# A triangle-multiplication layer and a gated row layer in one kernel: transfers of the opening reordered, stage-border copies and stores moved, one load split

## The chip, the cores and the metric

The kernel runs on one core of one Trainium2 chip. The metric is the device time of one execution in microseconds (us), and the median over several runs is compared. Profiles show one execution. TensorE (PE, with its weight loads PEld), VectorE (DVE), ScalarE (ACT) and GpSimd (POOL) compute; SyncE (SP) only issues transfers, and ScalarE and GpSimd can issue some too.

## The reference

The input x has 384 x 384 positions of 128 channels in float32. Two layers follow one another.

```python
def layernorm(x, g, b): ...                       # over the channels
z = layernorm(x, norm_g, norm_b)
left  = (z @ Wl + bl) * sigmoid(z @ Wlg + blg)
right = (z @ Wr + br) * sigmoid(z @ Wrg + brg)
core = einsum('bikh,bjkh->bijh', left, right)     # 128 products of 384 x 384 x 384
x1 = x + sigmoid(x @ Wg + bg) * (layernorm(core, onorm_g, onorm_b) @ Wout + bout)

l = x1 @ W_left + b_left + x1 @ W_eq + b_eq
rsum = sum over j of (x1 @ W_right + b_right)
u = l * rsum * sigmoid(x1 @ W_gate + b_gate)
y = layernorm(u @ W_out + b_out + x1, ln_scale, ln_bias)
```

## The kernel before, in words

The work runs in three stages, each bound to the order in which the program is written: every instruction goes through `seq`, so each engine executes its instructions in program order. Semaphores are set by the tile framework; a transfer waits for what it reads and for the buffer it overwrites.

**Stage 1 (0 to about 1140 us)** reads x in chunks of 8 rows i by 128 columns k (`load_chunk`, six buffers), computes mean and variance per position on VectorE (`stats`, lines 220 to 230), the power -1/2 on GpSimd (`powers`), the shifted rows z on GpSimd (`shift`), transposes them on TensorE and copies them with ScalarE (`front`, lines 258 to 264), and multiplies them with the joined weights `wz` (`back`, line 298). Four rows of a chunk are one step. The opening before the loop loads two chunks on SP; on ScalarE's queue it loads four weight matrices into `stage`, the norm's gain g and bias b as columns, the four bias vectors broadcast over the partitions, and four more chunks. `fold` (lines 152 to 156) and `weights` (line 162) fold gain and biases into `wz`: wz = g*W + bias/C + a mean of (b-g)*W, computed by one matmul p1.

**Stage 2 (about 1140 to 1885 us)** runs over the 128 values of h: it loads left and right of one h, forms the 384 x 384 product in PSUM (`pc`, line 449), copies it to `ct` with ScalarE, keeps sums over h for the second norm (`csum`, `csq`), and stores `ct` to the scratch tensor `core_d` in device memory, laid out [i, h, j]. The last h is treated by itself (lines 467 to 480): its first block of 128 rows is finished first, so that variance, square root, reciprocal and a Newton step (`variance`, `root`, `inverse`, `newton`) for rows 0 to 127 can run at once; the result is `roots[0][1]`, called r.

**Stage 3 (about 1885 us to the end)** runs over rows i in steps t, several rows in flight. Per row: the gate product (`front`, line 564), `scale_core` (cs = core times r: for rows 0 to 3 on VectorE, line 598, with r spread over the partitions by a matmul; later on GpSimd from `rt`, line 600), `layer0` (lines 609 to 612), `gated_left` (626 to 631), `layer1` (638, 639), statistics, normalization and store. Loads come in groups of four rows: `load_x`, `add_x` (a transfer issued by GpSimd that adds onto what `load_x` brought), and `load_core` (line 532 for `ct`, line 536 for `rt`). `store_rstd(0)` (line 557) writes r to device memory, from where `rt` reads it back. `pieces` are the variance and roots of row blocks 1 and 2, done a bit at a time between the rows: three variance operations or the like on ScalarE and GpSimd, or a reciprocal on VectorE.

The PSUM pools of stage 3 are `ps` (four banks) and `ps2` (four banks), opened in this order over the banks that stage 2 frees.

Of the kernel before, what the change touches and what calls it, by code (L numbers as in the profile page):

```python
# [8 lines left out]
F32 = mybir.dt.float32  # L9
# [10 lines left out]
def triangle_then_gated_row_kernel(ctx: ExitStack, tc: tile.TileContext, a: dict, out: bass.AP):  # L20
# [36 lines left out]
    def seq(ins):  # L57

        return tc.keep_in_program_order(ins)
# [7 lines left out]
    def column(name, queue=nc.sync):  # L67
        t = const([P, 1], "col_" + name)
        load(t, a[name].rearrange("(p o) -> p o", o=1), queue)
        return t  # L70
# [10 lines left out]
    with ExitStack() as ctx2:  # L81
# [15 lines left out]
        with tc.tile_pool(name="p1x", bufs=6, side="right") as xp, \  # L97
# [9 lines left out]
            loaded, normed = {}, {}  # L107
            lr, full = {}, []

            def load_chunk(n, queue=nc.sync):  # L110
                if n < len(chunks):
                    kb, ig, c = chunks[n]
                    i0 = ig * G + c * XR
                    xt = xp.tile([P, XR, C], F32, tag="xt", name="xt")
                    seq(queue.dma_start(
                        out=xt, in_=x[i0:i0 + XR, kb * P:(kb + 1) * P, :].rearrange("i k c -> k i c")
                    ))
                    loaded[n] = xt

            for n in range(2):  # L120
                load_chunk(n)

            stage = lrp.tile([P, H, G, 2], F32, tag="lr", name="stage").rearrange("p h i s -> p (h i s)")
            wst, bst = stage[:, 0:4 * H], stage[:, 4 * H:8 * H]
            m1, d = stage[:, 8 * H:9 * H], stage[:, 9 * H:9 * H + 1]
            sides = ("l", "r", "lg", "rg")
            for n, w in enumerate(sides):
                load(wst[:, n * H:(n + 1) * H], a["L0_conv_W" + w], nc.scalar)  # L130
            g0, b0 = column("L0_conv_norm_g", nc.scalar), column("L0_conv_norm_b", nc.scalar)
            for n, b in enumerate(sides):
                load(bst[:, n * H:(n + 1) * H], a["L0_conv_b" + b].partition_broadcast(P), nc.scalar)
            for n in range(2, 6):
                load_chunk(n, nc.scalar)
            ident = const([P, P], "ident")
            make_identity(nc, ident)
            avg = const([P, P], "avg")
            seq(nc.vector.memset(avg, 1.0 / P))
            mhalf = const([P, 16], "mhalf")  # L140
            seq(nc.vector.memset(mhalf, -0.5))

            warm = const([P, 1], "warm")
            seq(nc.scalar.activation(warm, mhalf[:, 0:1], AF.Sigmoid))
            wz = const([P, 4 * H], "wz")
            p1 = pps.tile([P, 2, 4 * H], F32, tag="pr", name="p1")[:, 0]

            def fold():

                seq(nc.vector.tensor_sub(d, b0, g0))
                seq(nc.vector.tensor_scalar(m1, avg, d, None, ALU.mult))
                seq(nc.tensor.matmul(p1, lhsT=m1, rhs=wst, start=True, stop=True))
                seq(nc.vector.tensor_scalar(bst, bst, 1.0 / C, None, ALU.mult))
                seq(nc.vector.scalar_tensor_tensor(wst, wst, g0, bst, ALU.mult, ALU.add))

            def weights():

                for g in range(2):  # L160
                    gs = slice(g * 2 * H, (g + 1) * 2 * H)
                    seq(nc.vector.tensor_add(
                        wz[:, gs].rearrange("p (h s) -> p s h", s=2),
                        wst[:, gs].rearrange("p (s h) -> p s h", s=2),
                        p1[:, gs].rearrange("p (s h) -> p s h", s=2),
                    ))

            wc = const([P, C], "wc")
# [154 lines left out]
            for k in range(AHEAD):  # L323
                for half in range(2):
                    stats(*steps[k], half)
                if k < AHEAD - 1:
                    powers(*steps[k])
                if k == 0:
                    fold()
                    zs[0] = shift(*steps[0])  # L330
                    front(*steps[0], zs.pop(0))
                if k == 1:
                    weights()
                    zs[1] = shift(*steps[1])
            for k, (n, q) in enumerate(steps):
                if k + 2 < len(steps):
                    zs[k + 2] = shift(*steps[k + 2])
                if k + AHEAD - 1 < len(steps):
                    powers(*steps[k + AHEAD - 1])
                for half in range(2):  # L340
                    back(n, q, half)
                    if half == 0 and k + 1 < len(steps):
                        front(*steps[k + 1], zs.pop(k + 1))
                    if k + AHEAD < len(steps):
                        stats(*steps[k + AHEAD], half)
                if q == NQ - 1:
                    del loaded[n], normed[n]
                    load_chunk(n + 6)
                    if chunks[n][2] == G // XR - 1:
                        store_nd(*chunks[n][:2])  # L350
                store_zt(n, q)
                store_slice()
                if k == 4:
                    for t, src in later:
                        load(t, src)
                if k == 20:
                    m2 = late_weights()
                if k == 21:
                    late_products(m2)
                if k == len(steps) - 2 * G // 4 + 16:  # L360
                    assert not full
                    for h in range(2):
                        load_h(h)
# [43 lines left out]
        with tc.tile_pool(name="p2r", bufs=2, side="right", reuse_waits="tile") as rrp, \  # L407
# [28 lines left out]
            for h in range(H):  # L436
# [20 lines left out]
                if h < H - 1:  # L457
                    seq(nc.scalar.copy(ct, pc[:, :, :N]))  # L458
                    seq(nc.scalar.activation(sq, ct, AF.Square))
                    seq(nc.vector.tensor_add(csum, csum, ct))  # L460
                    seq(nc.vector.tensor_add(csq, csq, sq))
                    load_h(h + 3)

                    queue = nc.sync if h < H - 3 else nc.scalar
                    seq(queue.dma_start(out=to, in_=ct))
                else:
                    seq(nc.scalar.copy(ct[:, 0], banks[0]))
                    seq(nc.scalar.activation(sq[:, 0], ct[:, 0], AF.Square))
                    seq(nc.scalar.dma_start(out=to[:, 0], in_=ct[:, 0]))
                    seq(nc.vector.tensor_add(csum[:, 0], csum[:, 0], ct[:, 0]))  # L470
                    seq(nc.vector.tensor_add(csq[:, 0], csq[:, 0], sq[:, 0]))
                    variance(0, slice(0, N))
                    root(0)
                    inverse(0, slice(0, N))
                    newton(0, slice(0, N))
                    seq(nc.scalar.copy(ct[:, 1:], pc[:, 1:, :N]))
                    seq(nc.scalar.dma_start(out=to[:, 1:], in_=ct[:, 1:]))
                    seq(nc.gpsimd.tensor_tensor(sq[:, 1:], ct[:, 1:], ct[:, 1:], ALU.mult))
                    seq(nc.gpsimd.tensor_tensor(csum[:, 1:], csum[:, 1:], ct[:, 1:], ALU.add))
                    seq(nc.gpsimd.tensor_tensor(csq[:, 1:], csq[:, 1:], sq[:, 1:], ALU.add))  # L480
# [5 lines left out]
    with ExitStack() as ctx3:  # L486
# [3 lines left out]
        xp, fp, inp, op = pool("p3x", 6), pool("p3f", A + 4), pool("p3in", 3), pool("p3out", 3)  # L490
        wp, sp = pool("p3w", 4), pool("p3s", 4)
        lp = pool("p3l", 11)
        ps, ps2 = pool("p3ps", 4, space=PSUM), pool("p3ps2", 4, space=PSUM)

        def bank(name):
            return ps.tile([P, 512], F32, tag="bank", name=name)
# [32 lines left out]
        def load_core(i0):  # L529
            if i0 < N:  # L530
                ct = inp.tile([P, RG, N], F32, tag="ct", name="ct")
                seq(nc.sync.dma_start(out=ct, in_=core_d[i0:i0 + RG].rearrange("i h j -> h i j")))
                rt = None
                if i0 > 0:
                    rt = inp.tile([P, RG, N], F32, tag="rt", name="rt")
                    seq(nc.sync.dma_start(
                        out=rt.rearrange("p i j -> p (i j)"),
                        in_=rstd_d[i0:i0 + RG].rearrange("i j -> (i j)").partition_broadcast(P),
                    ))
                cin[i0] = ct, rt  # L540
# [160 lines left out]
                ))  # L701
            stores.clear()

        for i0 in range(0, 4 * RG, RG):
            load_x(i0)
        load_core(0)
        store_rstd(0)
        load_core(RG)

        pieces = [(variance, b, s) for b in range(1, NB) for s in cols]  # L710
# [3 lines left out]
        for t in range(N + 3):  # L714
# [6 lines left out]
            if t >= 2 and fetched <= f + 16:  # L721
                load_x(fetched)
                fetched += RG
            if t >= 7 and added <= f + 8:
                add_x(added)
                added += RG
            if t < N:
                scale_core(t)
            if t >= 16 and t % 5 == 0 and pieces:
                step, b, s = pieces.pop(0)  # L730
                step(b, s)
                if step is root:
                    step, b, s = pieces.pop(0)
                    step(b, s)
                if step is newton and s == cols[-1]:
                    store_rstd(b)
# [70 lines left out]
```

## Time and profile before

| | us |
|---|---|
| median of three runs | 3308.44 (3307.75 to 3309.41) |
| the profiled execution | 3307.08 |
| its span (first to last instruction) | 3305.3 |
| granted TensorE clock | 0.997 of full speed |

The span is 1.8 us shorter than the execution's own time. The costliest groups of the page show how the time is spent:

```profile
L298 PE MATMUL pr<-wz,zt 128*128 128x512 f32 x2304 | 1040.3, 593 | 6.2 <-DVE st L228 6.2
L449 PE MATMUL pc<-rr,lrh 128*128 128x384 f32 x2304 | 745.0, 487 | 2.7 <-POOL rr L428 2.7
L600 POOL TENSOR_TENSOR cs<-ct,rt 128x384 f32<-128x384 f32 x380 | 403.7, 1064 | 10.4 <-DMA rt<-rstd_d 9.6
```

Such a line gives the source line, engine and operation, result and operands, shape and count; after the first bar the busy time in us and the mean of one in ns; after the second the idle time of the engine just before these instructions and what ended most of it. The chain of work that ended last is TensorE's almost throughout: line 449 alone is 22% of the span, and lines 638, 609, 627, 564 and 626 have about 7% each.

### The profile page before, as it was taken

The page shows a single profiled execution, that of the slowest core. Times are in us where ns is not written, and L with a number is a line of the kernel's source. Part 1 is how long each engine was busy: PE and PEld are TensorE (multiplying, and loading weights), DVE is VectorE, ACT ScalarE, POOL GpSimd, SP SyncE. Part 2 cuts the span into 40 slices and gives each one's busy share as a digit, 9 for nine tenths or more (in the row PEclk, how much of TensorE's full clock was granted, in tenths as well). Part 3 has the DMA queues.
Part 4 walks back from the last instruction along what each step waited for, and adds up shares of the span by engine and source line. Part 5 has one row for each costly group of instructions (what it writes and reads, how often), then busy time and mean ns, then how long its engine had stood idle before and what let it go on. Part 6 is the DMA issues. An engine that isn't in the chain of part 4 may idle for free.

```text
span 3305.3 us, 48361 instructions
## 1 busy us (share of the span) xinstructions
PE 3267.0 (99%) x12486; PEld 1992.0 (60%) x12486; DVE 2495.4 (75%) x8041; ACT 1940.4 (59%) x4055; POOL 2247.9 (68%) x3295
## 2 busy tenths in 40 slices
PE   8999999999999999999999999999999999999998
PEld 4544444444444466666666666666777777777776
DVE  6777777777777655555555688888888888888888
ACT  4555555555555433343334467777777777777776
POOL 5555555555555455555555579889888888888887
PEclk9999999999999999999999999999999999999999
DMA  5999999999999499999999999999999999999983
GB/s 151 267 281 268 266 279 272 264 282 271 263 279 275 130 283 283 283 281 283 284 283 282 287 296 267 264 273 276 269 280 270 275 271 276 273 272 277 271 258 113
DMA packets 922818, 873.96 MB, mean 264 GB/s; under 512 B 25008, under 2 KB 837680, under 8 KB 922544
## 3 DMA queue, kind: packets, MB, share of 16 engines
q1 hardware_dynamic: 902480, 794.13, 78.3%
q0 software_dynamic: 13248, 72.36, 11.1%
q10 hardware_dynamic: 6816, 4.39, 0.5%
q8 instruction: 102, 1.67, 0.2%
q14 instruction: 172, 1.41, 0.1%
HBM read 508.89 MB, written 361.89 MB: 263 GB/s over the span
## 4 chain that ended last, share of the span: by engine, by line
PE 62%; POOL 1%; ACT 1%; DVE 1%; issue 0%; POOLq 0%; DVEq 0%; ACTq 0%
PE pc L449 22%; PE py L638 7%; PE pr L609 7%; PE pl L627 7%; PE pg L564 7%; PE pg L626 7%; PE py L639 4%; POOL rs L658 0%; ACT py L673 0%; POOL yt L690 0%; PE pxt L575 0%; PE pq L586 0%; POOL cs L600 0%; DVE st L653 0%; ACT gT L566 0%
## 5 line engine op out<-in xcount | busy, mean ns | idle before, releaser
L298 PE MATMUL pr<-wz,zt 128*128 128x512 f32 x2304 | 1040.3, 593 | 6.2 <-DVE st L228 6.2
L305 ACT ACTIVATE sg<-pr,rs 128x256 f32<-128x256 f32 x1152 | 482.7, 470 | 499.2 <-PE pr L298 365.6
L449 PE MATMUL pc<-rr,lrh 128*128 128x384 f32 x2304 | 745.0, 487 | 2.7 <-POOL rr L428 2.7
L307 DVE SCALAR_TENSOR_TENSOR lr<-pr,rs,sg 128x256 f32<-128x256 f32 x1152 | 505.0, 480 | 267.2 <-ACT sg L305 218.8
L298 PEld LDWEIGHTS pr<-wz,zt 128*128 128x128 f32 x2304 | 414.4, 190 | 417.1 <-issue 346.0
L449 PEld LDWEIGHTS pc<-rr,lrh 128*128 128x128 f32 x2304 | 452.7, 197 | 295.0 <-POOL rr L428 3.3
L673 ACT ACTIVATE py<-py,nm,rs 128x128 f32<-128x128 f32 x1149 | 492.8, 429 | 191.6 <-POOL rs L662 126.9
L638 PEld LDWEIGHTS py<-wo,u 128*128 128x128 f32 x2304 | 377.1, 191 | 100.6 <-DVE yt L684 0.6
L460 DVE TENSOR_TENSOR csum<-csum,ct 128x1152 f32<-128x1152 f32 x127 | 175.6, 1383 | 346.6 <-ACT ct L458 346.6
L600 POOL TENSOR_TENSOR cs<-ct,rt 128x384 f32<-128x384 f32 x380 | 403.7, 1064 | 10.4 <-DMA rt<-rstd_d 9.6
L428 POOL COPY rr<-lrh 128x768 f32<-128x768 f32 x128 | 183.1, 1430 | 329.4 <-DMA lrh<-lr_d 309.2
L458 ACT COPY ct<-pc 128x1152 f32<-128x1152 f32 x127 | 142.1, 1119 | 449.4 <-PE pc L449 449.4
L638 PE MATMUL py<-wo,u 128*128 128x128 f32 x2304 | 402.7, 275 | 0.3 <-ACT wo L620 0.3
L690 POOL TENSOR_TENSOR yt<-yt,lnb 128x384 f32<-128x384 f32 x380 | 400.6, 1056 | 2.1 <-DVE yt L684 2.0
L653 DVE BATCH_NORM_STATS2 st<-py 128x6 f32<-128x128 f32 x1152 | 266.3, 287 | 84.6 <-PE py L639 82.9
L243 POOL TENSOR_SCALAR sd<-mv 128x8 f32<-128x8 f32 (+1 forms) x145 | 28.6, 197 | 436.7 <-DVE mv L230 436.6
L253 POOL TENSOR_TENSOR z<-xt,nd 128x512 f32<-128x512 f32 x288 | 299.8, 1041 | 35.9 <-POOL z L253 30.6
L609 PE MATMUL pr<-cs,wc 128*128 128x384 f32 x768 | 315.1, 492 | 0.1
L627 PE MATMUL pl<-x1T,mat_L_conv_W_left 128*128 128x384 f32 x768 | 311.4, 487 | 3.5 <-ACT gT L566 3.4
L639 PE MATMUL py<-ident,x1T 128*128 128x128 f32 x1152 | 314.0, 273 | 0.0
L626 PE MATMUL pg<-x1T,mat_L_conv_W_gate 128*128 128x384 f32 x768 | 310.8, 486 | 1.2 <-ACT g L629 1.0
L564 PE MATMUL pg<-xt,mat_L_conv_Wg 128*128 128x384 f32 x736 | 298.4, 487 | 0.0
(119 smaller groups left out, 4892.6 us busy)
## 6 DMA issues: line engine op xcount, KB each, us to landing
lr_d<-lr SPq DMA_DIRECT2D x128, 1024.0 KB, 7.1
lrh<-lr_d SPq DMA_DIRECT2D x128, 768.0 KB, 7.8
xt_d<-zt SPq DMA_DIRECT2D x288, 256.0 KB, 5.5
ct<-core_d SPq DMA_DIRECT2D x96, 768.0 KB, 4.8
rt<-rstd_d SPq DMA_DIRECT2D x95, 768.0 KB, 8.4
out_dram<-yt SPq DMA_DIRECT2D x94, 768.0 KB, 7.2
core_d<-ct SPq DMA_DIRECT2D x125, 576.0 KB, 8.9
xt<-in_x_dram SPq DMA_DIRECT2D x140, 512.0 KB, 7.0
```

The source lines that it names most:

```text
L298: seq(nc.tensor.matmul(pr[:, r, :], lhsT=zts[n, q][:, 2 * half + r, :], rhs=wz, start=True, stop=True))
L305: seq(nc.scalar.activation(sg[r], pr[:, r, 2 * H:], AF.Sigmoid, scale=rs[r]))
L307: seq(nc.vector.scalar_tensor_tensor(t[:, :, c * XR + r0 + r, :], pr[:, r, :2 * H].rearrange("k (h s) -> k h s", s=2), rs[r], sg[r].rearra ...
L449: seq(nc.tensor.matmul(banks[ib], lhsT=t[:, kb, ib * P:(ib + 1) * P, 0], rhs=rr[:, kb], start=(kb == 0), stop=(kb == NB - 1),))
L564: seq(nc.tensor.matmul(pg[:, :N], lhsT=wg0, rhs=r["xT"], start=True, stop=True))
L600: seq(nc.gpsimd.tensor_tensor(cs, ct[:, i % RG], rt[:, i % RG], ALU.mult))
L609: seq(nc.tensor.matmul(pr[:, :N], lhsT=wc, rhs=r["cs"], start=True, stop=True))
L626: seq(nc.tensor.matmul(pg2[:, :N], lhsT=wgate, rhs=r["x1T"], start=True, stop=True))
L627: seq(nc.tensor.matmul(pl[:, :N], lhsT=wleft, rhs=r["x1T"], start=True, stop=True))
L638: seq(nc.tensor.matmul(py[:, s], lhsT=r["u"][:, s], rhs=r["wo"], start=True, stop=False))
L639: seq(nc.tensor.matmul(py[:, s], lhsT=r["x1T"][:, s], rhs=ident, start=False, stop=True, is_transpose=True))
L673: seq(nc.scalar.activation(py[:, s], py[:, s], AF.Identity, bias=bias, scale=scale))
```

## The change

The edits fall into three places.

*Opening.* `load_chunk` can load a part of a chunk; SP loads the first four rows of chunk 0, then g and b as two rows of 128 numbers, the other four rows, and chunks 1 to 3. Chunks 4 and 5 are loaded after the first step of the loop. ScalarE's queue keeps the four weights only; the four bias vectors are loaded as one row each by GpSimd. `fold` stands between the two halves of the first statistics and brings g and b into columns by a small matmul with the identity; the bias goes into p1 by a second matmul with one row, and `weights` multiplies by g while adding p1. `busy` issues matmuls whose result nobody reads.

*Border between stages 2 and 3.* The first block's store of the last h is split into rows 0 to 3 and 4 to 127; ScalarE's copy of blocks 1 and 2 stands ahead of `variance` and `root`; r is stored by GpSimd's queue at this place instead of by SP in stage 3. The two PSUM pools of stage 3 change places. The core of rows 0 to 3 is loaded in two transfers, h 0 to 126 and h 127, and stands ahead of the fourth load of x.

*Row loop.* After t = 12 `add_x` is issued only where t mod 4 is 1, and pieces run where t mod 4 is 3, not where t is a multiple of 5.

```diff
-            def load_chunk(n, queue=nc.sync):
+            def load_chunk(n, part=slice(0, XR)):
...
-            for n in range(2):
-                load_chunk(n)
+            load_chunk(0, slice(0, 4))
...
+            for n, v in enumerate(("g", "b")):
+                load(gb[n:n + 1], a["L0_conv_norm_" + v].rearrange("(o h) -> o h", o=1))
             for n, w in enumerate(sides):
                 load(wst[:, n * H:(n + 1) * H], a["L0_conv_W" + w], nc.scalar)
-            g0, b0 = column("L0_conv_norm_g", nc.scalar), column("L0_conv_norm_b", nc.scalar)
-            for n, b in enumerate(sides):
-                load(bst[:, n * H:(n + 1) * H], a["L0_conv_b" + b].partition_broadcast(P), nc.scalar)
-            for n in range(2, 6):
-                load_chunk(n, nc.scalar)
+            load_chunk(0, slice(4, XR))
+            for n in range(1, 4):
+                load_chunk(n)
...
+            for n, b in enumerate(sides):
+                load(brow[:, n * H:(n + 1) * H], a["L0_conv_b" + b].rearrange("(o h) -> o h", o=1), nc.gpsimd)
...
+            def busy(n):
+
+                for _ in range(n):
+                    seq(nc.tensor.matmul(
+                        pb, lhsT=avg, rhs=avg.unsqueeze(1).to_broadcast([P, 4, P]), start=True, stop=True
+                    ))
...
-                seq(nc.vector.tensor_sub(d, b0, g0))
+                busy(2)
+                seq(nc.tensor.matmul(pgb, lhsT=gb, rhs=ident[0:2, 0:2], start=True, stop=True))
+                seq(nc.vector.tensor_copy(g0, pgb[:, 0:1]))
+                seq(nc.vector.tensor_sub(d, pgb[:, 1:2], g0))
                 seq(nc.vector.tensor_scalar(m1, avg, d, None, ALU.mult))
-                seq(nc.tensor.matmul(p1, lhsT=m1, rhs=wst, start=True, stop=True))
-                seq(nc.vector.tensor_scalar(bst, bst, 1.0 / C, None, ALU.mult))
-                seq(nc.vector.scalar_tensor_tensor(wst, wst, g0, bst, ALU.mult, ALU.add))
+                busy(1)
+                seq(nc.tensor.matmul(p1, lhsT=m1, rhs=wst, start=True, stop=False))
+                seq(nc.tensor.matmul(p1, lhsT=avg[0:1, :], rhs=brow, start=False, stop=True))
+                busy(1)
...
+                if k == 0:
+                    for i in range(4, 6):
+                        load_chunk(i)
...
-                    seq(nc.scalar.dma_start(out=to[:, 0], in_=ct[:, 0]))
+                    seq(nc.scalar.dma_start(out=to[:RG, 0], in_=ct[:RG, 0]))
+                    seq(nc.scalar.dma_start(out=to[RG:, 0], in_=ct[RG:, 0]))
...
+                    seq(nc.scalar.copy(ct[:, 1:], pc[:, 1:, :N]))
                     variance(0, slice(0, N))
                     root(0)
                     inverse(0, slice(0, N))
                     newton(0, slice(0, N))
-                    seq(nc.scalar.copy(ct[:, 1:], pc[:, 1:, :N]))
                     seq(nc.scalar.dma_start(out=to[:, 1:], in_=ct[:, 1:]))
+
+
+                    seq(nc.gpsimd.dma_start(out=rstd_d[0:P, :], in_=roots[0][1]))
...
-        ps, ps2 = pool("p3ps", 4, space=PSUM), pool("p3ps2", 4, space=PSUM)
+        ps2, ps = pool("p3ps2", 4, space=PSUM), pool("p3ps", 4, space=PSUM)
...
-                seq(nc.sync.dma_start(out=ct, in_=core_d[i0:i0 + RG].rearrange("i h j -> h i j")))
+
+                for hs in (slice(0, H),) if i0 > 0 else (slice(0, H - 1), slice(H - 1, H)):
+                    seq(nc.sync.dma_start(out=ct[hs], in_=core_d[i0:i0 + RG, hs].rearrange("i h j -> h i j")))
...
-        for i0 in range(0, 4 * RG, RG):
+        for i0 in range(0, 3 * RG, RG):
             load_x(i0)
         load_core(0)
-        store_rstd(0)
+        load_x(3 * RG)
         load_core(RG)
...
-            if t >= 7 and added <= f + 8:
+            if t >= 7 and (t % 4 == 1 or t < 12) and added <= f + 8:
...
-            if t >= 16 and t % 5 == 0 and pieces:
+            if t >= 16 and t % 4 == 3 and pieces:
```

More of the change, by code (lines that the diff above doesn't have):

```diff
@@ L113, in load_chunk @@
                     i0 = ig * G + c * XR
[L114 to L118, printed above, removed]
-            for n in range(2):
-                load_chunk(n)
+                    if part.start == 0:
+                        loaded[n] = xp.tile([P, XR, C], F32, tag="xt", name="xt")
+                    src = x[i0:i0 + XR, kb * P:(kb + 1) * P, :].rearrange("i k c -> k i c")
+                    seq(nc.sync.dma_start(out=loaded[n][:, part], in_=src[:, part]))
+            load_chunk(0, slice(0, 4))
             stage = lrp.tile([P, H, G, 2], F32, tag="lr", name="stage").rearrange("p h i s -> p (h i s)")
-            wst, bst = stage[:, 0:4 * H], stage[:, 4 * H:8 * H]
-            m1, d = stage[:, 8 * H:9 * H], stage[:, 9 * H:9 * H + 1]
+            wst, brow, gb = stage[:, 0:4 * H], stage[0:1, 4 * H:8 * H], stage[0:2, 8 * H:9 * H]
+            m1, d = stage[:, 9 * H:10 * H], stage[:, 10 * H:10 * H + 1]
             sides = ("l", "r", "lg", "rg")
+            for n, v in enumerate(("g", "b")):
+                load(gb[n:n + 1], a["L0_conv_norm_" + v].rearrange("(o h) -> o h", o=1))
             for n, w in enumerate(sides):
                 load(wst[:, n * H:(n + 1) * H], a["L0_conv_W" + w], nc.scalar)
-            g0, b0 = column("L0_conv_norm_g", nc.scalar), column("L0_conv_norm_b", nc.scalar)
-            for n, b in enumerate(sides):
-                load(bst[:, n * H:(n + 1) * H], a["L0_conv_b" + b].partition_broadcast(P), nc.scalar)
-            for n in range(2, 6):
-                load_chunk(n, nc.scalar)
-            ident = const([P, P], "ident")
-            make_identity(nc, ident)
+            load_chunk(0, slice(4, XR))
+            for n in range(1, 4):
+                load_chunk(n)
             avg = const([P, P], "avg")
@@ L141, in triangle_then_gated_row_kernel @@
             seq(nc.vector.memset(mhalf, -0.5))
+            ident = const([P, P], "ident")
+            make_identity(nc, ident)
+            for n, b in enumerate(sides):
+                load(brow[:, n * H:(n + 1) * H], a["L0_conv_b" + b].rearrange("(o h) -> o h", o=1), nc.gpsimd)
             warm = const([P, 1], "warm")
@@ L146, in triangle_then_gated_row_kernel @@
             p1 = pps.tile([P, 2, 4 * H], F32, tag="pr", name="p1")[:, 0]
+            pb = pps.tile([P, 2, 4 * H], F32, tag="pr", name="pb")[:, 0]
+            pgb = tps.tile([P, 4, P], F32, tag="pt", name="pgb")[:, 0, 0:2]
+            g0 = const([P, 1], "g0")
+            def busy(n):
[3 more added lines that the diff above has]
+                    ))
             def fold():
-                seq(nc.vector.tensor_sub(d, b0, g0))
+                busy(2)
+                seq(nc.tensor.matmul(pgb, lhsT=gb, rhs=ident[0:2, 0:2], start=True, stop=True))
+                seq(nc.vector.tensor_copy(g0, pgb[:, 0:1]))
+                seq(nc.vector.tensor_sub(d, pgb[:, 1:2], g0))
                 seq(nc.vector.tensor_scalar(m1, avg, d, None, ALU.mult))
-                seq(nc.tensor.matmul(p1, lhsT=m1, rhs=wst, start=True, stop=True))
-                seq(nc.vector.tensor_scalar(bst, bst, 1.0 / C, None, ALU.mult))
-                seq(nc.vector.scalar_tensor_tensor(wst, wst, g0, bst, ALU.mult, ALU.add))
+                busy(1)
+                seq(nc.tensor.matmul(p1, lhsT=m1, rhs=wst, start=True, stop=False))
+                seq(nc.tensor.matmul(p1, lhsT=avg[0:1, :], rhs=brow, start=False, stop=True))
+                busy(1)
             def weights():
@@ L161, in weights @@
                     gs = slice(g * 2 * H, (g + 1) * 2 * H)
-                    seq(nc.vector.tensor_add(
+                    seq(nc.vector.scalar_tensor_tensor(
                         wz[:, gs].rearrange("p (h s) -> p s h", s=2),
-                        wst[:, gs].rearrange("p (s h) -> p s h", s=2),
-                        p1[:, gs].rearrange("p (s h) -> p s h", s=2),
+                        wst[:, gs].rearrange("p (s h) -> p s h", s=2), g0,
+                        p1[:, gs].rearrange("p (s h) -> p s h", s=2), ALU.mult, ALU.add,
                     ))
@@ L325, in triangle_then_gated_row_kernel @@
                     stats(*steps[k], half)
+                    if k == 0 and half == 0:
+                        fold()
                 if k < AHEAD - 1:
@@ L328, in triangle_then_gated_row_kernel @@
                 if k == 0:
-                    fold()
                     zs[0] = shift(*steps[0])
+                    weights()
                     front(*steps[0], zs.pop(0))
                 if k == 1:
-                    weights()
                     zs[1] = shift(*steps[1])
```

## The prediction

> **What bounds the kernel now.** I read the page's busy table first, then the busy time by stage, TensorE's waits, and the order of time around the two places where TensorE stands idle.
>
> ```profile
> PE 3267.0 (99%) x12486; PEld 1992.0 (60%) x12486; DVE 2495.4 (75%) x8041; ACT 1940.4 (59%) x4055; POOL 2247.9 (68%) x3295
> ...
> 0.00:25.00 25.00, 9.96 (x22) 4.70 (x23) 11.56 (x64) 4.11 (x8) 10.48 (x23) 1.00 0.72 189
> ...
> 1880.00:1890.00 10.00, 7.60 (x29) 5.09 (x28) 7.89 (x9) 6.71 (x11) 2.06 (x2) 0.91 0.99 296
> ...
> 2020.00:2100.00 80.00, 77.38 (x367) 53.69 (x366) 66.67 (x239) 60.44 (x139) 68.72 (x95) 1.00 0.90 261
> 2100.00:2200.00 100.00, 98.48 (x470) 69.07 (x469) 87.43 (x305) 71.94 (x167) 89.46 (x127) 1.00 0.94 271
> ```
>
> The stage rows give the stretch, then busy us of PE, PEld, DVE, ACT, POOL. TensorE is idle 38 us of 3305.3. Of these 15.0 lie before 25 us, 2.4 at 1880 to 1890, 4.1 between 2020 and 2200, and about 14 after 3280, which nothing here touches. So the edits can win some 20 us at most, and only where TensorE waits; a new wait on its path costs its full length.
>
> ```profile
> 14.43 0.43 DVE L155 TENSOR_SCALAR stage<-stage 128x512 f32<-128x512 f32 x1 [5.63 <-DMA stage<-in_L_conv_brg_dram]
> 15.95 1.28 ACT L144 ACT_TABLE_LOAD   x1 [15.95 <-DMA xt<-in_x_dram]
> 17.35 0.57 ACT L264 COPY zt<-pt 128x512 f32<-128x512 f32 x1
> 17.97 3.55 PE L298 MATMUL pr<-wz,zt 128*128 128x512 f32 x4 [6.20 <-DVE st L228]
> ```
>
> In the opening two things are late together: the broadcast biases land at 14.4, so wz ends at 17.5; and ScalarE issues four x loads until 15.9, so its table load and the first copy zt end at 17.9. The first product starts at 17.97.
>
> ```profile
> 1887.91 2.55 PE L575 MATMUL pxt<-ident,xn 128*128 128x128 f32 x12 [2.40 <-ACT ct L476]
> 1889.55 1.05 SPq L532 DMA_DIRECT2D ct<-core_d  x1
> 1889.79 1.79 DVE L403 TENSOR_TENSOR r<-m 128x384 f32<-128x384 f32 x1
> 1893.70 0.56 DVE L405 SCALAR_TENSOR_TENSOR r<-r,m 128x384 f32<-128x384 f32 x1
> 1897.49 0.56 DVE L598 TENSOR_TENSOR cs<-ct,pb 128x384 f32<-128x384 f32 x1 [0.81 <-DMA rstd_d<-r]
> ```
>
> At the border TensorE waits 2.40 us for the last copy of pc. Then row 0's cs, at 1897.49, is the gate: the product with it, L610, L612 and the gate matmul at 1902.09 follow one another. It needs r (1894.26), the five copies L577 (to 1896.7) and ct. The core load's own row decides:
>
> ```profile
> ct<-core_d SPq DMA_DIRECT2D x1, 768.0 KB, 7.6
> ```
>
> Issued at 1889.55 plus 7.6 is 1897.15: the load lands last, so the wait named after rstd_d is really this transfer.
>
> [...] 12 transposes took 2.55 us above (213 ns each) and three take 0.33 (109 ns) once busy. [...] L403 took 1.79 us beside GpSimd's L478 and L479, against 0.56 for L405 of the same size.
>
> **The change, part by part.**
>
> *Opening.* Four 64 KB bias broadcasts become rows of 0.5 KB on GpSimd's queue, ScalarE issues only the four weights, x goes out on SP, and chunk 0 in halves. The bias is added by a second matmul onto p1, L155 and L156 go, and four dummy matmuls on avg keep TensorE busy. New order: x's first half and g, b land near 4 (an estimate from the whole chunk's landing at 5.4); two dummies (2.07 us each cold, from L154) end at 5.1; pgb, g0, d, m1 end near 6.5. The weights landed at 7.9 before behind 1 MB of x; they still share with 1 MB, so p1 starts at 7.9. Two matmuls at 0.9 end near 9.7, wz takes 0.72: 10.4. Beside it, half 1's statistics end at 7.3 (they stand behind m1 on VectorE), powers take 1.95, z 1.04: 10.3. Transposes 0.45 behind the last dummy, copy 0.57: first product at 11.6, 6.3 earlier than 17.97. The following ones are warm, but GpSimd then is late: z of step 1 at 14.6 (stats 1.2, powers 1.95, z 1.04 after wz), against 19.95 before, where cold products held TensorE to 21.36. The regular rhythm, at 21.80 before, starts near 15.1. Gain 6.5. GpSimd's four issues (about 1 us each, by L524's 0.91) end near 5.4, ahead of its first powers at 7.3, so they cost nothing; if the bias rows land after 8.8, each us is lost. Bounds 4.5 to 8. Chunks 4 and 5 now go out after the first store of zt, at about 12; they are needed at k=2, near 23.
>
> *Border, small parts.* The copy of pc's blocks 1 and 2 goes ahead of root: 1885.6 to 1886.4, and root, waiting for ve until 1886.6, loses nothing. Swapping the PSUM pools puts the first transposes on banks that copy does not read, so they may start at 1885.5. The store of rstd goes to GpSimd's queue ahead of sq, csum, csq: these wait for r, so Newton runs unhindered (0.56 instead of 1.79 and 2.05), r at 1891.5 instead of 1894.26. Behind that wait stand only L478 to L480 (5.3 us of GpSimd) and row 4's cs, which ran at 1902.9; csum is not read before t=19. The copies L577 then end at 1894.0. All this moves row 0's gate from 1897.49 to 1894.7 at best, if ct lands by then.
>
> *Border, the split load.* ct of rows 0 to 3 becomes a 127-partition transfer and a 1-partition one; it is ahead of the fourth x load and does not wait for row block 0 of the last h. Its wait, the store of h=126, landed at 1888.7 (1880.9 + 7.8), so it is issued only some 1 us earlier. Its bytes are 127 x 4 x 1536 = 780,288. [...] What an engine moves: two windows,
>
> ```profile
> DMA packets 678, 0.35 MB, mean 347 GB/s; under 512 B 1, under 2 KB 678, under 8 KB 678
> ...
> DMA packets 2316, 2.11 MB, mean 352 GB/s; under 512 B 61, under 2 KB 2316, under 8 KB 2316
> ```
>
> (1889 to 1890 and 1891 to 1897; the best slices of the latter near 400) make 22 to 25 GB/s each of 16. I take 24: 32.5 us. The engine has first to finish the third x load, which landed at 1891.7 (1880.8 + 10.9). Landing 1924.2: row 0's cs moves from 1897.49 to 1924.3, +26.8. [...] TensorE, idle over 20 us, restarts cold (0 to 2, taken 1). Together +28.8. The gains of the small parts are inside this stall and are worth nothing. Bounds of the stall: 28.5 us at 27.4 GB/s (the best slice seen at 1880 to 1890, 438 GB/s, over 16) from 1890.5 gives +21.5; 17.5 GB/s (the stage's 280 over 16) gives 44.6 us, +39. Behind it on SP stand the fourth x load and ct, rt, xt of the next rows: seven loads of 2.5 us, landed by cs0 + 19, where the accumulating load of t=7 needs them at about cs0 + 20 (row 7's product ran at 1920.4, 22.9 after row 0's cs, and cs and the accumulating issue come before it); no further stall, by a small margin. [...]
>
> *Row loop.* Issues of the accumulating load move from t%4=0 to t%4=1, pieces from every fifth t to t%4=3.
>
> ```profile
> 2028.51 0.92 POOL L524 DMA_DIRECT2D xt<-xt_d  x1
> 2030.18 0.70 POOL L380 TENSOR_TENSOR ve<-ve,m 128x128 f32<-128x128 f32 x1
> ...
> 2036.83 0.91 PE L627 MATMUL pl<-x1T,mat_L_conv_W_left 128*128 128x384 f32 x2 [1.23 <-ACT gT L566]
> ```
>
> Here both fell into t=40 ahead of the pair's powers (every even t), and 1.23 us were lost; a like stall of 1.5 lies near t=80. They can no longer meet. Against it, a Newton piece (three of 0.46 to 0.71) every fourth step fills GpSimd more densely: four steps of 3.58 us are 14.3, and hold four cs and four yt of 1.0, two power chains of 2.2, the issue of 0.9 and the piece of some 1.7, together 15.0. The two table loads of root (1.0 lost near 2065) remain. Net -1.2, bounds -3 to +1.5.
>
> **Sum.** -6.5 + 28.8 - 1.2 = +21.1 on the profiled 3307.1: 3328.2. The median of the runs shown is 1.4 above that execution: 3329.5.
>
> **Rivals.** *The load spreads over all engines after all.* The instruction would then be the 768 KB load of before, minus one x load ahead of it: 1897.15 less 2.5 is 1894.6, and the gate moves by -2.8. Sum -6.5 - 2.8 - 1.2 = -10.5: 3298. For it: the old load took 7.6 us. [...] The point that decides is whether the landing stays under some 12 us. Chance 0.13. *The split costs and the opening gives nothing,* because bias rows or GpSimd's powers come late: 3336, still slower, inside the main case's chance. *Partial spread* or a stall of about 10 us cancelling the rest: 3308, chance 0.02.
>
> **How the numbers follow.** Slower by one engine 0.85, spread 0.13, level 0.02. A difference under 0.2% (6.6 us) cannot be told from none. The first case's own range, the extremes not all together, is 3317 to 3346 and holds 0.95 of its 0.85, which is 0.81; so the range needs no reach to 3298.
>
> **What would show it.** Right: ct<-core_d of the first rows landing some 30 us or more after issue, VectorE's L598 idle over 20 us on that transfer, one gap of TensorE of that length near 1885 to 1915; the first L298 near 11.6; the wait at 2036 gone. Wrong: a landing under 10 us, with TensorE busy throughout the border.

## The result, and the profile after

The changed kernel takes 3330.27 us (median of six runs, 3329.64 to 3333.10), the one before 3307.82 (six runs, 3307.12 to 3309.41): a ratio of 1.0068, interval 1.0055 to 1.0081, or 22.4 us more. The forecast was 3329.5. The profiled execution of the changed kernel is the slowest of its six (3333.1, span 3331.2), so the two spans differ by 25.9. That execution lies 2.8 us above the median, about what its opening lost (below).

The page of the changed kernel, busy table and slices of the span (each slice is 83 us):

```profile
PE 3276.3 (98%) x12498; PEld 1994.3 (60%) x12498; DVE 2483.5 (75%) x8040; ACT 1940.3 (58%) x4055; POOL 2254.3 (68%) x3300
...
PE   9999999999999999999999689999999999999998
...
DMA  5998998998998499999999689999999999999993
```

TensorE now lacks 54.9 us of its span instead of 38.3, and the slices say where: one slice stands at 6, the 23rd, near 1830 to 1915, and the transfers stand at 6 in the same one. The busy time by stage (stretch; sum; busy us of PE, PEld, DVE, ACT, POOL; granted clock, share of the DMA engines, GB/s) narrows it:

```profile
0.00:25.00 25.00, 22.38 (x50) 9.66 (x51) 14.34 (x77) 6.50 (x14) 15.80 (x31) 0.86 0.74 192
...
1875.00:1885.00 10.00, 9.12 (x37) 5.56 (x36) 7.40 (x8) 8.10 (x13) 0.06 (x1) 1.00 0.92 273
1885.00:1920.00 35.00, 6.35 (x29) 3.63 (x27) 4.38 (x9) 4.43 (x8) 5.66 (x4) 0.63 0.22 71
1920.00:1945.00 25.00, 20.99 (x67) 12.50 (x68) 13.54 (x29) 8.19 (x16) 7.83 (x8) 0.83 0.94 324
```

Between 1885 and 1920 every engine is almost still, and so are the DMA engines, at 71 GB/s. Nobody is busy, so the wait looks like one for something narrow. The order of time around it:

```profile
1884.19 29.58 SPq L557 DMA_DIRECT2D ct<-core_d  x2
1885.32 0.56 DVE L422 TENSOR_TENSOR r<-m 128x384 f32<-128x384 f32 x1
...
1887.36 0.67 POOL L500 DMA_DIRECT2D rstd_d<-r  x1 [12.30 <-DVE r L424]
...
1913.81 0.44 SPq L533 DMA_DIRECT2D xn<-in_x_dram  x1
...
1923.23 1.02 DVE L623 TENSOR_TENSOR cs<-ct,pb 128x384 f32<-128x384 f32 x2 [33.07 <-DMA ct<-core_d]
1923.84 1.65 PE L589 MATMUL pg<-xT,mat_L_conv_Wg 128*128 128x384 f32 x2 [32.01 <-DVE cs L623]
...
1930.06 0.91 PE L651 MATMUL pg<-x1T,mat_L_conv_W_gate 128*128 128x384 f32 x2 [0.17 <-DVE x1T L637]
```

r has long been there (its store starts at 1887.36), but row 0's cs waits 33.07 us for the two loads of the first rows' core, and TensorE 32.01 us behind it. The second line shows a Newton operation at 0.56 us, where the same one (L403) took 1.79 before. What the DMA engines did in the stall, seen from 1895 to 1912:

```profile
DMA packets 267, 0.41 MB, mean 24 GB/s; under 512 B 0, under 2 KB 267, under 8 KB 267
...
q1 hardware_dynamic: 267, 0.41, 6.6%
```

A share of 6.6% is about what one of 16 engines busy without pause would give (6.25%); 0.41 MB move in 17 us, 24 GB/s, in packets of one row of j (1536 B). The opening, for comparison with the first product at 17.97 before:

```profile
9.86 1.89 PE L155 MATMUL pb<-avg 128*128 128x512 f32 x2
...
13.28 3.77 PE L313 MATMUL pr<-wz,zt 128*128 128x512 f32 x4 [0.67 <-ACT zt L279]
...
17.32 3.60 PE L313 MATMUL pr<-wz,zt 128*128 128x512 f32 x8
```

The profile counts each of these float32 matmuls as two records: L154 of the kernel before, one matmul, stands there as x2. The regular rhythm (eight records in a row of 3.60) starts at 17.32 instead of 21.80. In the profiles of the six other kernels below with this very opening it starts between 14.4 and 15.0, and the first product at 11.0 to 11.4 (forecast: 15.1 and 11.6). In this execution the bias rows landed late (TensorE waited 0.91 us for them), the dummy matmul behind them ran slowly, cold in the prediction's word (1.89 us for its two records, 1.13 in the profile of the one-load kernel below), and so did the first products (3.77 for four records, half the speed of the line below). The granted clock of this profile stood at 0.50 from 11.7 to 15 us and at 1.00 from 17 to 18. The 2.3 to 2.9 us lost so are of the size of the 2.8 by which this execution is above its median.

So the spans' difference adds up by place. The end of stage 2 comes at 1881.03 instead of 1885.51: -4.5. From there to row 0's gate matmul (L651, L626 before) it takes 49.0 us instead of 16.6: +32.4. From there to the end 1401.1 instead of 1403.2: -2.1. Sum +25.8, with rounding the 25.9 seen.

### The profile page after: what moved, and what is told of

The parts are those of the page before. It is cut to its first block, busy times and chain, and to the rows that moved or that the text cites. A ratio compares the mean times of both kernels' runs of the same rounds, so it can differ in the third digit from the quotient of the medians.

```text
span 3331.2 us, 48399 instructions
## 1 busy us (share of the span) xinstructions
PE 3276.3 (98%) x12498; PEld 1994.3 (60%) x12498; DVE 2483.5 (75%) x8040; ACT 1940.3 (58%) x4055; POOL 2254.3 (68%) x3300
## 4 chain that ended last, share of the span: by engine, by line
PE 95%; POOL 1%; SPq 1%; DMA 1%; DVE 1%; ACT 1%; issue 0%; POOLq 0%; ACTq 0%
PE pr L313 30%; PE pc L468 22%; PE py L663 7%; PE pr L634 7%; PE pl L652 7%; PE pg L651 7%; PE pg L589 7%; PE pt L277 4%; PE py L664 4%; SPq L557 1%; POOL rs L683 0%; POOL cs L625 0%; POOL yt L715 0%; ACT py L698 0%; DMA rt<-rstd_d 0%
## 5 line engine op out<-in xcount | busy, mean ns | idle before, releaser
L625 POOL TENSOR_TENSOR cs<-ct,rt 128x384 f32<-128x384 f32 x380 | 428.4, 1129 | 39.0 <-DMA rt<-rstd_d 37.2
L479 DVE TENSOR_TENSOR csum<-csum,ct 128x1152 f32<-128x1152 f32 x127 | 177.6, 1399 | 353.3 <-ACT ct L477 353.3
L715 POOL TENSOR_TENSOR yt<-yt,lnb 128x384 f32<-128x384 f32 x380 | 425.3, 1120 | 3.4 <-DVE yt L709 3.2
L268 POOL TENSOR_TENSOR z<-xt,nd 128x512 f32<-128x512 f32 x288 | 300.4, 1043 | 34.6 <-POOL z L268 29.3
L652 PE MATMUL pl<-x1T,mat_L_conv_W_left 128*128 128x384 f32 x768 | 311.5, 487 | 1.2 <-ACT gT L591 1.2
L651 PE MATMUL pg<-x1T,mat_L_conv_W_gate 128*128 128x384 f32 x768 | 310.8, 486 | 1.1 <-ACT g L654 0.9
```

The costliest lines, as they stand in the source:

```text
L625: seq(nc.gpsimd.tensor_tensor(cs, ct[:, i % RG], rt[:, i % RG], ALU.mult))
L651: seq(nc.tensor.matmul(pg2[:, :N], lhsT=wgate, rhs=r["x1T"], start=True, stop=True))
L652: seq(nc.tensor.matmul(pl[:, :N], lhsT=wleft, rhs=r["x1T"], start=True, stop=True))
```

## The experiments

Two theories stood against each other: the split load runs through one DMA engine (the author's assumption, which no load of the kernel before could show), or the stall has another cause at this border (the load's new place in SP's queue, r's store on GpSimd, two transfers instead of one). Every kernel was timed beside the kernel before, whose median was 3306.4 to 3306.6.

**The changed kernel with the first rows' core in one load.**

```diff
-                for hs in (slice(0, H),) if i0 > 0 else (slice(0, H - 1), slice(H - 1, H)):
+                for hs in (slice(0, H),):
```

> The changed kernel, with the core of rows 0 to 3 loaded in one transfer of 128 partitions again, at its new place ahead of the fourth x load. One-engine theory: the load lands within about 8 us of its issue, the 32 us gap of TensorE is gone, and the time is 3296 to 3301, faster than before by 0.2 to 0.35%. Rival, that the stall comes from the new place and the new waits of the load and of r's store on GpSimd's queue: the time stays at 3325 to 3332.

Measured: 3295.08 (3293.82 to 3297.24), ratio to the kernel before 0.9967, interval 0.9954 to 0.9979; this is 0.9 us below the expected range. All other edits stay in place, so the stall needs the split, and this kernel beats both. In the order of time around the border of this kernel:

```profile
1881.56 0.37 SPq L557 DMA_DIRECT2D ct<-core_d  x1
...
1887.36 0.56 DVE L602 COPY xT<-pxt 128x384 f32<-128x384 f32 x1 [1.33 <-PE pxt L600]
...
1888.88 0.55 DVE L623 TENSOR_TENSOR cs<-ct,pb 128x384 f32<-128x384 f32 x1 [0.96 <-DMA xn<-in_x_dram]
```

The issue takes 0.37 us instead of holding SP for 29.58. Its row gives the time to landing:

```profile
ct<-core_d SPq DMA_DIRECT2D x1, 768.0 KB, 7.2
```

So the load lands at 1888.76, 0.12 us before row 0's cs, and the core is still the last arrival. The name in brackets, the third load of x, is not what was missing: VectorE's copy L602 of row 8, whose transposes wait for that load, ended at 1887.92, and the matmul that spreads r for row 0 (pb) at 1887.97. Row 0's cs runs 10.75 us after the end of stage 2 (at 1878.13), against 11.98 before: measured from that end the load is issued 0.6 us earlier (3.4 after it instead of 4.0), and it takes 7.2 us instead of 7.6.

**The kernel before with nothing but the split.**

```diff
-                seq(nc.sync.dma_start(out=ct, in_=core_d[i0:i0 + RG].rearrange("i h j -> h i j")))
+                for hs in (slice(0, H),) if i0 > 0 else (slice(0, H - 1), slice(H - 1, H)):
+                    seq(nc.sync.dma_start(out=ct[hs], in_=core_d[i0:i0 + RG, hs].rearrange("i h j -> h i j")))
```

> The kernel before with nothing but the split into 127 and 1. One-engine theory: the load starts on its engine after the fourth x load, at about 1895, and takes 32.5 us; row 0's cs comes about 30 us later than before, and SP, held by the issue, stores r and loads its copies later as well: 3337 to 3345. Rival, that the split alone is harmless and the stall needs the other edits at the border: 3305 to 3310.

Measured: 3338.24 (3337.56 to 3338.84), ratio 1.0096, interval 1.0082 to 1.0110. The order of time of this kernel:

```profile
1887.30 30.38 SPq L533 DMA_DIRECT2D ct<-core_d  x2
...
1926.88 1.02 DVE L599 TENSOR_TENSOR cs<-ct,pb 128x384 f32<-128x384 f32 x2 [31.48 <-DMA rstd_d<-r]
```

The stall comes without any other edit. The wait is put down to r's store, which here stands behind the split loads on SP and so starts only at 1917.72; cs does not read it. Between 1900 and 1917 the DMA engines move 25 GB/s as above: the name in brackets is not always the operand that was missing.

**The split after h 111, in 112 and 16 partitions.** The edit is `slice(0, H - 16), slice(H - 16, H)` in the line above, in the changed kernel.

> The changed kernel, split into 112 and 16 values of h: still two transfers at the same place. One-engine theory: both use 16 engines, 3296 to 3301, the same as the whole load or up to 1 us better, since the first part has no wait on the last stores of h. Rival, that two transfers or their place cost the stall: 3325 to 3332.

Measured: 3298.14 (3293.40 to 3299.49), ratio 0.9972, interval 0.9962 to 0.9982. Both parts are multiples of 16, and there is no stall to speak of:

```profile
1890.77 1.02 DVE L623 TENSOR_TENSOR cs<-ct,pb 128x384 f32<-128x384 f32 x2 [2.76 <-DMA ct<-core_d]
```

This cs comes 12.15 us after the end of stage 2 (at 1878.62), much as in the kernel before (11.98). So two transfers in place of one do not make the stall; it is the size of the part. The 3.1 us above the kernel with one load lie within overlapping intervals.

**The split in 126 and 2**, with `slice(0, H - 2), slice(H - 2, H)`.

> The changed kernel, split into 126 and 2 values of h in place of 127 and 1. One-engine theory: 126 is divisible by 2, so two engines carry 387 KB each; at 24 GB/s that is 16.1 us against 32.5, and the time falls by about 16 us to 3312 to 3316. If any outer size that is no multiple of 16 costs the same, or if the stall comes from there being two transfers: 3328 to 3332.

Measured: 3297.51 (3293.09 to 3298.90), ratio 0.9970, interval 0.9958 to 0.9982. The expectation missed by some 15 us, and the mistake was in its arithmetic, not in the theory: it took 2 for the number of engines, but the largest number up to 16 that divides 126 is 14. Corrected so, the theory puts the part on 14 engines, nearly the width of a whole load, and expects no such stall; in this trace VectorE waited 2.6 us before row 0's cs and TensorE 1.5 us behind it. How many engines carried the part was not seen. That leaves the theory resting on 127 alone, so two sizes with few divisors followed.

**The splits in 122 and 6, and in 124 and 4.** 122 is 2 x 61, its largest divisor up to 16 is 2; that of 124, 4 x 31, is 4.

> The changed kernel, split into 122 and 6 values of h. The largest divisor of 126 up to 16 is 14, not 2, which is why the 126 split cost nothing; 122 is 2 times 61, so its largest is 2. One-engine theory in its general form (the number of engines is the largest divisor up to 16): 374,784 B on each of two engines at 24 GB/s take 15.6 us against 32.5 for 127, so the time is 16.9 us under the changed kernel's 3330.3: 3311 to 3316. Rival, that only an odd or prime size is slow, or that 127 is a special case: 3295 to 3299.

> The changed kernel, split into 124 and 4 values of h. General theory: 4 engines, 190,464 B each, 7.9 us, so 24.6 us under the changed kernel's 3330.3, 3303 to 3308, part of it hidden behind the other inputs of row 0's cs, so 3300 is possible. Rival of a special 127: 3295 to 3299.

Measured: 3312.59 (3311.24 to 3315.54), ratio 1.0019, interval 1.0012 to 1.0026, for 122; 3307.99 (3305.89 to 3309.49), ratio 1.0003, interval 0.9995 to 1.0012, for 124. Row 0's cs of the kernel with 122:

```profile
1874.47 18.24 SPq L557 DMA_DIRECT2D ct<-core_d  x2
...
1902.31 1.02 DVE L623 TENSOR_TENSOR cs<-ct,pb 128x384 f32<-128x384 f32 x2 [16.73 <-DMA ct<-core_d]
```

and of the kernel with 124:

```profile
1874.66 10.86 SPq L557 DMA_DIRECT2D ct<-core_d  x2
...
1896.71 1.02 DVE L623 TENSOR_TENSOR cs<-ct,pb 128x384 f32<-128x384 f32 x2 [10.96 <-DMA ct<-core_d]
```

An `x2` of SPq spans both issues and the wait between them. In their stalls the DMA engines moved 45 to 50 GB/s with 122, and 88 GB/s with 124 (1892 to 1894, at a share of 27.2% where four engines of 16 would be 25%): some 22 to 25 GB/s for each unit of the divisor. The whole row of sizes:

| first part | largest divisor up to 16 | median, us | GB/s in the stall |
|---|---|---|---|
| 127 | 1 | 3330.3 | 24 |
| 122 | 2 | 3312.6 | 45 to 50 |
| 124 | 4 | 3308.0 | 88 |
| 126 | 14 | 3297.5 | no stall |
| 112 | 16 | 3298.1 | no stall |

The larger part is not the slower one; among these five sizes the divisor orders the stalls. The stalls of 122 and 124 flatter their widths a little: these loads do not need the store of h=126 and are issued 2 us before the end of stage 2, against 3 us after it with 127.

**The opening alone, on the kernel before.** The edit is the first place of the diff, all of it.

> The kernel before with the edits of the opening alone. Theory: the regular rhythm of stage 1 starts near 14.7 as in the last four kernels and not at 20.5 to 21.8, 6 to 7 us gained: 3300 to 3301 beside 3306.6 of before. Rival, that the gain of the opening is only the 4.5 us which the changed kernel's own profile shows: 3302.

Measured: 3300.13 (3298.67 to 3300.76), ratio 0.9979, interval 0.9970 to 0.9987: -6.3 us. The rhythm starts at 14.59 in its profile. The prediction had 6.5 and 15.1.

**The one-load kernel without the dummy matmuls.**

```diff
-                busy(2)
...
-                busy(1)
...
-                busy(1)
```

> The changed kernel with the whole load and without the four dummy matmuls. If they matter by keeping the clock up, the matmuls of p1, the first transposes and the first products take twice as long, and the rhythm starts some 2 to 3 us later: 3297 to 3298 beside 3295. If they don't, or if the last one only delays the transposes by standing ahead of them: 3294 to 3295.

Measured: 3299.24 (3298.70 to 3300.64), ratio 0.9978, interval 0.9970 to 0.9986: 4.2 us above the one-load kernel, from two groups of runs with nearly the same time of the kernel before (3306.42 and 3306.55). The expectation had 2 to 3 us. In the two profiled executions, whose own times differ by 2.9, the end of stage 2 lies 2.9 us later (1881.02 against 1878.13). Its first products, in order of time:

```profile
12.34 3.78 PE L310 MATMUL pr<-wz,zt 128*128 128x512 f32 x4 [0.68 <-DVE st L240]
15.91 1.06 PE L274 MATMUL pt<-ident,z 128*128 128x128 f32 x4
```

and those of the one-load kernel with the dummies:

```profile
11.15 1.98 PE L313 MATMUL pr<-wz,zt 128*128 128x512 f32 x4 [0.68 <-ACT zt L279]
```

Four records take 3.78 us without the dummies and 1.98 with them; the two matmuls of p1 take 2.05 and 2.07 without and 1.02 and 1.12 with them. The changed kernel's own profile fits: there the dummies ran, TensorE waited 0.91 us for a late transfer ahead of the last of them, and the four records took 3.77 at a granted clock of 0.50. That the clock is the cause was not shown for the opening: in the kernel before four records took 3.55 us at a reading of 1.00 (17.9 to 21.3 us). Without the dummies 4.2 of the opening's 6.3 us are gone by the medians, 2.9 by the profiles.

**The two row-loop edits alone, on the kernel before.**

```diff
-            if t >= 7 and added <= f + 8:
+            if t >= 7 and (t % 4 == 1 or t < 12) and added <= f + 8:
...
-            if t >= 16 and t % 5 == 0 and pieces:
+            if t >= 16 and t % 4 == 3 and pieces:
```

> The kernel before with the two edits of the row loop alone. Theory: the collision of the accumulating issue with a piece at t=40 and t=80 goes, 1 to 3 us gained: 3304 to 3306 beside 3306.6. Rival, that the denser pieces load GpSimd more and give it back: 3306.5 to 3308.

Measured: 3304.29 (3303.63 to 3305.54) beside 3306.41, ratio 0.9994, interval 0.9986 to 1.0002. The 2.1 us lie inside what the interval leaves open, so the time alone does not show a gain. TensorE's waits (total us, times, longest) have this line in the kernel before and in this kernel:

```profile
PE pl L627 <- ACT gT L566: 3.4, 4, 1.5
...
PE pl L627 <- ACT gT L566: 1.2, 4, 0.3
```

So the two stalls named in the prediction are gone, worth 2.2, and this agrees with the median.

**The border edits alone, on the kernel before, with the core in one load.** The edit is the second place of the diff, with the loop over `hs` reduced to `(slice(0, H),)`.

> The kernel before with the edits of the border alone, the first core load whole. Theory: row 0's cs comes 1.2 us earlier against the end of stage 2, as in the run with the whole load, up to the predicted 2.8: 3304 to 3305.5 beside 3306.6. Rival, that the border's small parts give nothing because the DMA queues are full there in any order: 3306 to 3307.

Measured: 3305.57 (3304.80 to 3307.02) beside 3306.41, ratio 0.9998, interval 0.9990 to 1.0006. This is -0.8, between the two expectations and not to be told from none. In its trace row 0's cs comes 10.34 us after the end of stage 2 (at 1884.68), 1.6 earlier than before, and the core lands 0.4 us ahead of it: this load is the last arrival here too. What keeps it from landing earlier was not tested.

The parts add up to -6.3 - 2.1 - 0.8 = -9.2; together, without the split, they measured -11.5. The 2.3 between is within the spread of these medians.

## Why the prediction was right

**The split load: right in its mechanism, 3.6 us short in size.** That a load of 127 partitions goes through one engine was the author's assumption, which the trace of before could not show. The runs fit it: 24 GB/s with 127, 45 to 50 with 122, 88 with 124, and no such stall with 126 and 112. The rate of one engine, 24 GB/s, was an estimate from the full width (347 to near 400 GB/s over 16); the stall measured 24. That the load moves its bytes only behind the third x load was an estimate too. The landing was mis-sized: row 0's cs was put 38.8 us after the end of stage 2 (1924.3 less 1885.5) and came 42.2 after it. Of these 3.4 us, 1.8 lie in the start, the third load of x, which landed 8.0 us after the end of stage 2 (at 1889.05, when its transposes went on) and not 6.2. The other 1.6 lie in the load itself: from there to cs it takes 34.2 us, against the 32.6 that the prediction left (32.5 for the bytes at 24 GB/s, and 0.1 to cs). The 1 us that the prediction set aside, as an estimate, for the load of the last h behind it covers part of this; the two transfers' landings are not told apart. The last term, a cold restart, was taken at 1 us and is about 2.2: the gate matmul came 32.45 later while cs came 30.2 later, with products of 1.65 and 1.40 us instead of 0.81. The granted clock stood at 0.50 from 1895 to 1928 and at 1.00 from 1929 to 1931.

**Hidden border gains: right.** Newton at 0.56 us and r at 1887.1 were worth nothing beside a cs at 1923.2. One reading was off: beside the slow L403 GpSimd ran L479 and L480; L478 had ended 0.4 us before it began.

**The opening: right.** -6.3 measured alone against -6.5. The profiled execution gave only -4.5, the lower bound, by the late bias rows that the prediction had named as its risk.

**The row loop: right, 0.9 us short in size.** -2.1 in the trace and in the runs, within the bounds of -3 to +1.5 around -1.2; the denser pieces cost nothing to be seen. In the changed kernel's waits the line `pl L652 <- ACT gT L591` has the same 1.2 us, longest 0.3.

**The rival of the load that spreads** was excluded by the 24 GB/s. Its time, 3298, is near that of the kernel with one load (3295.1), but its border term was too large: it moved the gate by -2.8, where the two kernels with the whole load show -1.2 and -1.6 in their traces and -0.8 in the runs. The step that failed there took 2.5 us off the landing, for the x load that no longer stood ahead. Measured from the end of stage 2 the core landed 10.6 and 10.0 us after it in these two kernels, against 11.6 before: only 1.0 and 1.7 us earlier, and it was still the last arrival.

**By the median:** -6.3 + 32.4 - 2.1 = +24.0 from the parts, and +22.4 measured. The difference of 1.6 stays open. That the forecast of 3329.5 met the median within 0.8 us is in part luck: the split cost 3.6 us more than its term, the row loop gave 0.9 more, 1.6 of the parts' sum is missing from the median, and the kernel before took 0.6 us less over six runs than over the three that the forecast started from.

## What to carry to other kernels

Before splitting a transfer, work out the largest divisor up to 16 of each part's outermost size, which ordered the stalls of the five sizes measured here: 127 + 1 of 128 turned a load for which VectorE waited 0.8 us into one for which it waited 33, while 126 + 2 and 112 + 16 made no such stall. When all engines and the DMA engines are idle together, look at the DMA share: here 6.6%, about one sixteenth, without pause was a single load at 24 GB/s. And undo the parts one at a time: here the rest of the change (0.33% faster, interval 0.21% to 0.46%) was buried under one bound of a slice.

## What the hardware showed unexpectedly

A slow load held the queue that issued it. By the chain of waits SP's first issue took 0.27 us, but the one behind it, of only 6 KB, 29.26; so the fourth load of x went out at 1913.81 and r's store, when it stood there (the split alone), at 1917.72. The hold shrank with the width of the first part: the second issue took 29.3 us with a divisor of 1, 12.8 with 2, 5.7 with 4, 0.7 with 14 and 0.3 with 16. And an opening with the same instructions started its rhythm anywhere between 14.4 and 17.3 us, and in the latest of them a transfer of 0.5 KB had landed late (a wait of 0.91 us) and the matmuls behind it ran cold (3.77 us for four records, at a granted clock of 0.50); that the one caused the other was not tried, and in the profile of the opening alone TensorE waited 0.74 us for a weight matrix and stayed warm (1.98 us for four records).
